# First layer's votes: nine taps in 128 + 32 contraction rows for the upper half of each tile, the seventh share in one PSUM bank, and a new order

## The chip, the cores and the metric

The kernel runs on one core of a Trainium2 chip. The metric is the device time in microseconds (us) of one execution. A core has a tensor engine (PE, with its weight loads listed apart as PEld), a vector engine (DVE), a scalar engine (ACT), GpSimd (POOL) and a sync engine (SP), which only issues transfers here. Each takes its instructions in order from its own queue; engines wait for each other on semaphores. Matrix products land in PSUM, eight banks of 128 x 512 float32; PE writes there, DVE and ACT read from there. All else on chip lies in SBUF.

## The reference, cut to what matters

Four layers, each `x = x + layer(groupnorm(x))` on x of 8 images, 16 channels, 256 x 256 pixels. Only layer 0, a convolution with three rounds of routing, is touched:

```python
w = weights.reshape(kh, kw, cin, atoms * cout)          # 3, 3, 16, 8 * 16
votes = conv_general_dilated(tensor, w, (1, 1), 'SAME')  # 8 * 16 = 128 outputs per pixel
votes = votes.reshape(n, atoms, cout, h, wdt)            # a b c d e, a = image
logits = zeros((a, b, d, e))
for _ in range(3):
    r = softmax(logits, axis=0)                          # over the 8 images
    preds = squash(einsum('abcde,abde->bcde', votes, r), axis=0)
    logits = logits + einsum('abcde,bcde->abde', votes, preds)
return preds
```

Nine taps of 16 channels make 144 contraction rows for 128 outputs. The weighted sum over images, the squash (a norm over the atoms), the dot product with the votes and the softmax over images follow, for every pixel.

## The kernel before, in words

Layer 0 (`layer0`) walks the image in 64 tiles of four rows. A tile has an upper half (h=0, rows 4i and 4i+1) and a lower half (h=1); a half has two rows j; the eight images of a row go in two groups g of four. `prepare` makes the normalised input of a tile: x into `xs`, a product with `wd` (L479, into `pd`), ACT adds the bias (L482, `dn`), and the tile goes to a padded scratch array `d0` in HBM. The output of the first product of a tile lies 128 partitions (8 atoms x 16) by 512 (two rows of 256 pixels) per image, `v[h]`.

Votes before, for both halves: `kt[h]` holds four rows x 16 channels, twice, the second copy shifted by one pixel (dx), so 128 partitions. One call `votes(h, j, g)` makes four images of a row: two matmuls of 128 contraction rows (dx=0 and 1, L533) and two of 64 rows (dx=2, L537; one in each half of the array's rows), into a pair of banks `cv`; ACT copies them to `v` (L542). A row uses three of the four loaded rows, so a quarter of the weights are zeros. Eight calls make a tile: 16 + 16 matmuls.

Then, three times: `squash` (squares on ACT L569, sums over atoms on PE L573, root on ACT L587 to L589, division on DVE L593 to L595, one product on POOL L599 into `f`). After the first two: `logits` for each half: `factor` spreads `f` to 128 rows (PE L617, into a pair of banks `fb`), DVE scales it (L635), multiplies the votes of four and of three images with it (L643, `pr`), PE sums over the output channels (L653, `pl`); `softmax` (transposes L700, L724; DVE L706 to L707 and L716 to L718; exp on ACT L712); `weighted`: PE spreads the shares `rs` of seven images to 128 rows (`rb`, L751: images 4, 5 and 6 in one call, 0 to 3 in another), DVE multiplies them with the votes (L762, `dd`, three pairs and a single one per half), POOL adds up (L771). At the end DVE scales (L813), POOL adds x (L816, `res`), ACT measures sums for the next layer (L828), SP stores (L839, L840, L846 or L848).

What sets the order: layer 0's operations are first recorded, then `_Order.run` writes them out. Each operation has a rank, tile number times a period (61.05) plus an entry of the list `TIMES`; of those whose inputs are recorded as made and whose buffers are free, the lowest rank comes next. The list thus gives priorities, not times: on the chip an instruction starts when its engine and its semaphores let it. About three tiles are in flight. Buffers are counted by kind: three pairs of PSUM banks `x` (for `pd`, `cv`, `fb`, `rb`) and two single banks `u` (for the squash's sums `n2`, `pl`, and the transposes `lg`, `rt`); `kt` has two buffers, `v` six, `dd` four, `io` one (`xs` and `res` share it). Buffers of a kind go round: the next user of a place waits until the last reader of the earlier one is done.

Of the kernel before, what the change touches and what calls it, by code (L numbers as in the profile page):

```python
# [18 lines left out]
P = 128  # L19
WP = W + 2  # L20
# [10 lines left out]
def _consts():  # L31

    p = np.arange(P)
    hi, lo = p // 16, p % 16

    fold = np.stack([h * 16 + lo[:, None] == np.arange(32)[None, :] for h in range(2)], 1)
    unfold = np.zeros((4, 2, C, 2, 4, P), np.float32)
    for h in range(2):
        for k in range(4):
            unfold[k, h, :, h, k] = 0.5 * (np.arange(C)[:, None] == lo[None, :])  # L40


    sel = np.stack([16 * g + 8 * h + hi[:, None] == np.arange(32)[None, :] for g in range(2) for h in range(2)], 1)
    spread = np.zeros((4, 2, 2, 8, 2, 2, 8, C), np.float32)
    for g in range(2):
        for h in range(2):
            for b in range(8):
                spread[:, g, h, b, g, h, b] = 1.0

    diff = np.zeros((B, C, C, B), np.float32)  # L50
    for i in range(C):
        for a in range(B - 1):
            diff[a, i, i, a] = 1.0
            diff[B - 1, i, i, a] = -1.0
        diff[:, i, i, B - 1] = 1.0 / B
    parts = {

        "pair": 0.5 * (p[:, None] // 2 == p[None, :] // 2),
        "diff": diff.reshape(P, P),

        "fold": fold.reshape(P, 2 * 32),
        "unfold": unfold.reshape(P, 8 * P),

        "sel": sel.reshape(P, 4 * 32),

        "spread": spread.reshape(P, 4 * P),
        "ident": np.eye(P),

        "group": (lo[:, None] // 2 == lo[None, :] // 2) / 16.0,

        "same_lo": lo[:, None] == lo[None, :],
        "ones": np.ones((P, P)),
        "mean": np.full((P, P), 1.0 / P),

        "same_c4": lo[:, None] == p[None, :] % 64 // 4,

        "hi8": hi[:, None] == np.arange(8)[None, :],
        "row0": p[:, None] == np.arange(16)[None, :],

        "middle": -(p[:, None] % 4 - 1.5),  # L80

        "pad": _padding(),


        "keep": np.stack([p >= 16, (p < 48) | (p >= 64), p >= 64, p < 64], 1),

        "ident3": _ident3(),
    }
    at = 0
    cols = []  # L90
    for name, a in parts.items():
        a = np.asarray(a, np.float32)
        _CONST[name] = (at, a.shape[1])
        at += a.shape[1]
        cols.append(a)
    return np.ascontiguousarray(np.concatenate(cols, 1))
# [39 lines left out]
def _layout(w0, bw, sw, sc, bias, wq, bq, wk, bk, wv, bv, w3):  # L136
# [1 line left out]


    w0 = w0.reshape(3, 3, C, P)  # L140
    l0 = np.zeros((2, 2, 4, C, 2, P), np.float32)
    for j in range(2):
        for kh in range(3):
            for dx in range(2):
                l0[0, dx, j + kh, :, j] = w0[kh, dx]
                l0[1, dx, j + kh, :, j] = w0[kh, 2]
    l0 = l0.reshape(2, P, 2 * P).transpose(1, 0, 2)


    sw = sw.transpose(1, 4, 2, 3, 0).reshape(C, 2, 4, 81 * C).transpose(0, 2, 1, 3).reshape(64, 2 * 81 * C)  # L150
# [28 lines left out]
class _Buf:  # L179
# [10 lines left out]


TIMES = [
    -723.29, -126.96, -1287.20, -291.27, -719.97, -693.08, -625.75, -683.80, -169.92, -158.78, -153.36,
    -1032.45, -146.30, -286.26, -145.45, -1375.99, -151.90, -338.16, -261.20, -230.76, -136.99, -214.63,
    -126.67, -136.17, -143.63, -139.13, -140.10, -174.81, -899.84, -137.38, -135.05, -211.64, -133.88, -127.93,
    -109.08, -115.69, -139.61, -115.29, -118.15, -149.20, -107.32, -110.73, -165.19, -382.13, -97.75, -92.86,
    -92.25, -91.12, -89.08, -198.43, -88.34, -238.75, -240.66, -85.79, -84.47, -254.75, -133.10, -336.72,
    -223.36, -77.68, -126.26, -82.81, -264.25, -217.14, -78.43, -75.92, -107.53, -72.84, -47.31, -266.51,
    -185.51, -154.67, -555.69, -72.72, -216.04, -93.74, -182.88, -41.32, -30.68, -276.56, -149.62, -123.61,
    -28.12, -118.42, -27.48, -29.71, -88.26, -84.70, -24.63, -62.07, -138.31, -998.81, -338.10, -23.75, -71.35,  # L200
    -168.85, -21.77, -17.87, -1189.68, -15.52, -17.81, -78.48, -11.77, 13.13, -11.07, 16.57, -105.36, -162.33,
    31.16, -216.22, 15.81, 16.90, 16.88, -188.95, 24.25, 29.14, 26.46, 33.82, -255.28, -124.68, -124.23,
    -285.23, -135.30, -169.10, -92.14, -167.00, 36.88, -40.85, -558.24, -220.65, -113.85, -402.73, -159.96,
    35.14, -89.25, 53.60, 71.24, -670.06
]


# [79 lines left out]
class _Net:  # L287
# [123 lines left out]
    def layer0(self, wd, bd, less0, tiles=range(TILES)):  # L411
# [8 lines left out]
        with ExitStack() as st:  # L420
# [1 line left out]
            self.constants(one, "fold", "ident")  # L422
            sbuf = st.enter_context(tc.tile_pool(name="l0_sb", bufs=2))
            psum = st.enter_context(tc.tile_pool(name="l0_ps", bufs=1, space=PSUM))
            w = one.tile([P, 2, 2, P], F32, name="w0")
            nc.sync.dma_start(out=w.rearrange("p s j m -> p (s j m)"), in_=self.d["l0"].rearrange("p s f -> p (s f)"))
            tiny = one.tile([P, 1], F32, name="tiny")
            nc.vector.memset(tiny, 1e-18)
            stats = self.const.tile([P, 2, 2 * TILES], F32, name="st1")
            ident = self.k["ident"]  # L430
            fold = self.k["fold"].rearrange("p (h m) -> p h m", h=2)
            unfold = self.k["unfold"].rearrange("p (h k m) -> p h k m", h=2, k=4)
            sel = self.k["sel"].rearrange("p (g h m) -> p g h m", g=2, h=2)
            spread = self.k["spread"].rearrange("p (g h m) -> p g h m", g=2, h=2)
            ROW = P * WP
# [16 lines left out]
                )  # L452
            nc.sync.dma_start(out=self.d0[(H + 2) * ROW :].unsqueeze(0), in_=ring[0][0:1, 0, 0:16])

            places = dict(io=1, kt=2, v=6, sq=2, f=2, ls=3, e=2, rs=2, s=3, pr=2, dd=4)
            banks = dict(x=3, u=2)
            order = _Order({**places, **banks}, 61.05, TIMES)

            def buf(kind, shape, name=None):
                pool = psum if kind in banks else sbuf  # L460
# [36 lines left out]
            def work(i):  # L497
# [6 lines left out]
                if i + 2 < TILES:  # L504
                    prepare(i + 2, op)

                kt = [buf("kt", [P, 8 * WP]) for _ in range(2)]
                for h in range(2):
                    for dx in range(2):

                        def fetch(h=h, dx=dx):
                            at = (4 * i + 2 * h) * ROW + dx
                            nc.sync.dma_start(
                                out=kt[h]()[dx * 64 : dx * 64 + 64],
                                in_=self.d0[at : at + 4 * ROW].rearrange("(p f) -> p f", f=8 * WP),
                            )

                        op("SP", 0.5, fetch, [("d0", i), ("d0", i + 2 * h - 1)], [(kt[h], dx)], lag=6.0)
                res = buf("io", [P, 2, 512], "res")


                v = [buf("v", [P, 8, 512]) for _ in range(2)]

                def votes(h, j, g):


                    ps = buf("x", [P, 2, 512], "cv")

                    def products():
                        t = kt[h]().rearrange("p (a w) -> p a w", a=8)  # L530
                        for n in range(2):
                            a = 4 * g + 2 * n
                            nc.tensor.matmul(ps()[:, n], w[:, 0, j, :], t[:, a : a + 2, 0:W], start=True, stop=False)  # L533
                        for n in range(2):
                            a = 4 * g + 2 * n
                            at = slice(n * 64, n * 64 + 64)
                            nc.tensor.matmul(  # L537
                                ps()[:, n], w[at, 1, j, :], t[at, a : a + 2, 2 - n : 2 - n + W], start=False, stop=True
                            )

                    def move():
                        nc.scalar.copy(  # L542
                            v[h]()[:, 4 * g : 4 * g + 4, j * W : j * W + W],
                            ps().rearrange("p n (a w) -> p (n a) w", w=W),
                        )

                    op("PE", 3.2, products, [(kt[h], 0), (kt[h], 1)], [(ps, 0), (v[h], "turn")], mode="votes")
                    op("ACT", 1.1, move, [(ps, 0)], [(v[h], g, j)])

                def voted(h, a):  # L550
                    return [(v[h], a // 4, 0), (v[h], a // 4, 1)]

                for g in (1, 0):
                    for h in range(2):
                        for j in range(2):
                            votes(h, j, g)

                def rows(ap):
                    return ap.rearrange("p (r w) -> p r w", w=W)
# [46 lines left out]
                def factor(f, h, also=()):  # L606
# [4 lines left out]
                    def products():  # L611
                        for b in also:
                            b()
                        for n in range(2):
                            for j in range(2):
                                at = slice(64 * j, 64 * j + 64)
                                nc.tensor.matmul(  # L617
                                    fb()[:, j, n * P : n * P + P],
                                    unfold[at, h, 2 * j + n, :],
                                    f()[at, 3],  # L620
                                    start=True,
                                    stop=True,
                                )
# [112 lines left out]
                def weighted(rs):  # L736
# [3 lines left out]
                    for h in range(2):  # L740

                        def term(images, h=h):

                            rb = [buf("x", [P, 2, 512], "rb") for _ in images]

                            def products():
                                for pair, r in zip(images, rb):
# [982 lines left out]
```

## Time and profile before

| what | value |
|---|---|
| time, three runs | median 6453.93 us (6452.06 to 6459.32) |
| profiled execution | 6451.19 us, its span 6448.7 us |
| granted PE clock, mean | 0.989 |
| busy in the span: PE / DVE / ACT / POOL | 6078.3 / 5060.9 / 2967.9 / 3394.3 us |
| votes of layer 0 on PE, first to last | 121.6 to 3369.8 us |
| PE busy, 1000 to 2000 us | 957.96 us |
| DVE busy, 1000 to 2000 us | 894.92 us |
| POOL and ACT busy, 1000 to 2000 us | 759.34 and 423.75 us |
| DMA share and rate, 1000 to 2000 us | 0.37, 96 GB/s |

The profile is one execution on the chip. A row of a table by groups names line, engine, operation, output and input, the number of instructions, their busy time and mean length, then the idle time of the engine ahead of them with what ended it. A float32 matmul shows as two records. Busy shares are means over a stretch; what a stage costs is read from the waits in that stage. Layer 0 repeats with the tile: in a stretch of whole tiles each number divided by the tiles is that of one tile.

### The profile page before, as it was taken

The numbers are of one execution on the slowest core, as the hardware profiler recorded it, in microseconds if no ns is written. First come the engines' busy times: TensorE is split into PE (matmuls) and PEld (weight loads), VectorE is DVE, ScalarE is ACT, GpSimd is POOL, SyncE is SP. The second block draws the span as 40 slices with busy tenths as digits, with TensorE's granted clock in tenths as the row PEclk, the third lists the DMA queues.
The fourth block names the chain that finished last, engine by engine and source line by source line (L and its number), as shares of the span: only waits on it lengthen the run. The fifth ranks groups of instructions, "written<-read, shape, count | busy, mean of one in ns | idle before, by whom it ended". The sixth has DMA issues, their size and how long they took to land.

```text
span 6448.7 us, 109346 instructions
## 1 busy us (share of the span) xinstructions
PE 6078.3 (94%) x44488; PEld 2716.0 (42%) x44488; DVE 5060.9 (78%) x5963; ACT 2967.9 (46%) x4474; POOL 3394.3 (53%) x2464
## 2 busy tenths in 40 slices
PE   2999999999999999999995999999999999999998
PEld 1333333333333333333332444444444566666653
DVE  5788888888888888888886999999999633333331
ACT  0344444444444444444433888888888422112221
POOL 0577777777777777777775434334433211111123
PEclk9999999999999999999996999999999999999999
DMA  7333333333333333333323555555556543434358
GB/s 270 77 94 99 98 98 92 92 98 93 100 96 100 92 92 98 92 101 94 100 69 95 184 180 173 175 178 174 176 180 179 158 82 90 89 83 93 90 176 267
DMA packets 379593, 800.62 MB, mean 124 GB/s; under 512 B 57426, under 2 KB 191154, under 8 KB 343890
## 3 DMA queue, kind: packets, MB, share of 16 engines
q1 hardware_dynamic: 335250, 730.35, 40.4%
q0 software_dynamic: 9856, 29.20, 1.6%
q10 hardware_dynamic: 33984, 34.08, 1.5%
q8 instruction: 349, 5.72, 0.4%
q14 instruction: 154, 1.26, 0.1%
HBM read 582.77 MB, written 210.77 MB: 123 GB/s over the span
## 4 chain that ended last, share of the span: by engine, by line
PE 58%; DVE 32%; issue 4%; DMA 3%; ACT 1%; POOL 1%; SPq 0%; DVEq 0%; POOLq 0%; ACTq 0%
PE cv L533 13%; PE cv L537 7%; PE pqk L1455 7%; DVE bases L1009 7%; PE pl L653 6%; PE rb L751 5%; DVE e L999 4%; DVE pr L643 4%; PE po L1482 4%; DVE dd L762 4%; PE psc L1470 3%; PE pv L1462 3%; PE p L1547 3%; DVE a L999 2%; DVE a L978 2%
## 5 line engine op out<-in xcount | busy, mean ns | idle before, releaser
L771 POOL TENSOR_TENSOR dd<-dd 128x1024 f32<-128x1024 f32 x512 | 1209.0, 2361 | 338.7 <-DVE dd L762 318.4
L1032 PE MATMUL ps<-bases,tw 128*32 128x512 f32 (+1 forms) x13824 | 1361.7, 545 | 16.7 <-POOL bases L1001 6.7
L762 DVE SCALAR_TENSOR_TENSOR dd<-rb,v 128x1024 f32<-128x1024 f32 (+1 forms) x1024 | 1078.0, 1084 | 214.3 <-PE rb L751 175.5
L1001 POOL TENSOR_TENSOR bases<-e,a 128x1024 f32<-128x1024 f32 (+1 forms) x264 | 621.7, 2378 | 928.1 <-DVE e L999 927.8
L542 ACT COPY v<-cv 128x1024 f32<-128x1024 f32 x512 | 518.7, 1013 | 1281.2 <-PE cv L537 1281.2
L643 DVE TENSOR_TENSOR pr<-v,fb 128x2048 f32<-128x2048 f32 (+1 forms) x512 | 1010.9, 2015 | 32.0 <-PE pl L653 28.1
L533 PE MATMUL cv<-kt,w 128*128 128x512 f32 x2048 | 1009.1, 615 | 11.2 <-DMA kt<-d 9.4
L1032 PEld LDWEIGHTS ps<-bases,tw 128*32 128x32 f32 x13824 | 598.2, 109 | 801.7 <-issue 482.9
L771 POOL TENSOR_TENSOR s<-s,dd 128x512 f32<-128x512 f32 x512 | 653.3, 1276 | 30.1
L751 PE MATMUL rb<-rs,ct_fold 32*128 32x512 f32 x3584 | 605.6, 649 | 9.1 <-ACT rs L733 2.4
L533 PEld LDWEIGHTS cv<-kt,w 128*128 128x128 f32 x2048 | 347.0, 189 | 558.8 <-issue 392.7
L537 PE MATMUL cv<-kt,w 64*128 64x512 f32 x2048 | 578.8, 641 | 0.0
L653 PE MATMUL pl<-pr,ct_fold 128*32 128x512 f32 x3584 | 531.6, 605 | 45.4 <-DVE pr L643 45.2
L1466 ACT ACTIVATE vt<-pv,w_b2v 128x128 f32<-128x128 f32 x512 | 146.5, 368 | 840.2 <-PE pv L1462 840.2
L771 POOL TENSOR_TENSOR s<-v,dd 128x512 f32<-128x512 f32 x256 | 325.9, 1273 | 340.0 <-DVE dd L762 330.9
L1455 PE MATMUL pqk<-w_qk,t 128*128 128x512 f32 x1024 | 482.9, 594 | 4.7 <-POOL t L1449 4.6
L1487 DVE TENSOR_TENSOR y<-po,res 128x512 f32<-128x512 f32 x128 | 88.5, 691 | 493.9 <-PE po L1482 468.5
L1009 DVE SCALAR_TENSOR_TENSOR bases<-xr,xm,bases 128x1024 f32<-128x1024 f32 (+1 forms) x264 | 447.9, 1734 | 0.3 <-POOL bases L1001 0.3
L1449 POOL TENSOR_TENSOR t<-t,emb 128x512 f32<-128x512 f32 x128 | 162.5, 1270 | 514.0 <-DVE t L1445 494.3
L986 ACT ACTIVATE sq<-a 128x1024 f32<-128x1024 f32 (+1 forms) x264 | 263.7, 999 | 231.4 <-DVE a L978 230.7
L968 ACT ACTIVATE d<-xr,bd,sd 128x1024 f32<-128x1024 f32 (+1 forms) x264 | 319.0, 1208 | 14.1 <-DMA xr<-x1p 14.1
L751 PEld LDWEIGHTS rb<-rs,ct_fold 32*128 32x128 f32 x3584 | 173.0, 185 | 351.0 <-issue 118.2
(269 smaller groups left out, 8430.3 us busy)
## 6 DMA issues: line engine op xcount, KB each, us to landing
kt<-d SPq DMA_DIRECT2D x256, 516.0 KB
xr<-x1p SPq DMA_DIRECT2D x120, 1024.0 KB
d<-dn ACTq DMA_DIRECT2D x64, 516.0 KB
x<-y SPq DMA_DIRECT2D x128, 258.0 KB
xs<-in_x_dram SPq DMA_DIRECT2D x16, 2048.0 KB
xs<-in_x_dram SPq DMA_DIRECT2D x64, 512.0 KB
res<-in_x_dram SPq DMA_DIRECT2D x64, 512.0 KB
x<-s SPq DMA_DIRECT2D x128, 256.0 KB
```

The costliest lines, as they stand in the source:

```text
L533: nc.tensor.matmul(ps()[:, n], w[:, 0, j, :], t[:, a : a + 2, 0:W], start=True, stop=False)
L537: nc.tensor.matmul(ps()[:, n], w[at, 1, j, :], t[at, a : a + 2, 2 - n : 2 - n + W], start=False, stop=True)
L542: nc.scalar.copy(v[h]()[:, 4 * g : 4 * g + 4, j * W : j * W + W], ps().rearrange("p n (a w) -> p (n a) w", w=W),)
L643: nc.vector.tensor_tensor(pr()[:, :n].rearrange("p n (r w) -> p n r w", w=W), v[h]()[:, 4 * g : 4 * g + n].rearrange("p n (r w) -> p n r w ...
L653: nc.tensor.matmul(pl()[at : at + 32], sel[:, g, h, :], pr()[:, t, :], start=h == 0 and g == 0, stop=h == 1 and (g == 1 or t == 3),)
L751: nc.tensor.matmul(r()[:, n], spread[at, g, h, :], rs()[at], start=True, stop=True)
L762: nc.vector.scalar_tensor_tensor(dd()[:, :n], r()[:, :n], 1.0 / B, v[h]()[:, a : a + n], ALU.subtract, ALU.mult)
L771: op("POOL", us, lambda: nc.gpsimd.tensor_tensor(out[0](), a[0](), b[0](), ALU.add), a[1] + b[1], out[1])
L1001: nc.gpsimd.tensor_tensor(ring[n % 3][:, 0, p : p + m, 1 : 1 + W], rows(e), rows(a), ALU.subtract)
L1009: nc.vector.scalar_tensor_tensor(r, rows(part[1]), xm[:, b : b + 1], v, ALU.is_gt, ALU.mult)
L1032: nc.tensor.matmul(out if k is None else out[:, k], lhs, rhs, start=start, stop=stop, skip_group_check=True)
L1455: nc.tensor.matmul(ps, t[:, n, k * P : (k + 1) * P], wqk[:, n, :], start=n == 0, stop=n == 1)
```

## The change

Three things change in layer 0; the other layers are the same.

1. The upper half's votes. `kt` is now made per row j: partitions 0 to 95 hold three taps of dx=0 and three of dx=1, 96 to 127 two taps of dx=2 (16 channels each). A second, small buffer `kr` holds what the ninth tap needs, in four groups of 32 partitions, each with the two images of one matmul; half of the weights' rows there are zeros. The ninth tap's four matmuls of 32 rows come first and start all four banks of two `x` pairs (operation `rest`); then the eight taps' matmuls of 128 rows add to them (`most`, two per pair). The lower half keeps the old form under the name `votes_wide`. Fetches of the upper half per tile: six (two of 96 partitions, two of 32, two of `kr`) in place of two of 64.
2. The weighted sum's seventh image takes one `u` bank (`r6`) in place of a pair `x`.
3. Period and `TIMES` are new (49), and votes of a tile are recorded half by half.

The unused half of the constant `unfold` is dropped and the weight array `l0` carries both forms.

```diff
-            places = dict(io=1, kt=2, v=6, sq=2, f=2, ls=3, e=2, rs=2, s=3, pr=2, dd=4)
+            places = dict(io=1, kt=2, kr=2, v=6, sq=2, f=2, ls=3, e=2, rs=2, s=3, pr=2, dd=4)
             banks = dict(x=3, u=2)
-            order = _Order({**places, **banks}, 61.05, TIMES)
+            order = _Order({**places, **banks}, 49, TIMES)
...
+                def votes(h, j):
+                    kt = buf("kt", [P, 8 * WP])
+                    kr = buf("kr", [P, 2 * WP])
+                    at = (4 * i + 2 * h + j) * ROW
...
+                    def fetch():
+                        rows_at(kt()[:96], 0, [[1, 2], [8 * WP, 48], [1, 8 * WP]])
+                    def fetch2():
+                        rows_at(kt()[96:], 2, [[8 * WP, 32], [1, 8 * WP]])
+                    def fetch3():
+                        rows_at(kr(), 16 * 8 * WP + 2, [[2 * WP, 4], [8 * WP, 32], [1, 2 * WP]])
...
+                    ps = [buf("x", [P, 2, 512], "cv") for _ in range(2)]
+                    def most(g):
+                        t = kt().rearrange("p (a w) -> p a w", a=8)
+                        for n in range(2):
+                            a = 4 * g + 2 * n
+                            nc.tensor.matmul(ps[g]()[:, n], w[:, 0], t[:, a : a + 2, 0:W], start=False, stop=True)
+                    def rest():
+                        for g in range(2):
+                            for n in range(2):
+                                at = slice(64 * g + 32 * n, 64 * g + 32 * n + 32)
+                                t = kr()[at].rearrange("p (a w) -> p a w", a=2)[:, :, 0:W]
+                                nc.tensor.matmul(ps[g]()[:, n], w[at, 1], t, start=True, stop=False)
...
-                for g in (1, 0):
-                    for h in range(2):
+                for h in range(2):
+                    if h in (0,):
                         for j in range(2):
-                            votes(h, j, g)
+                            votes(h, j)
+                    else:
+                        wide(h)
...
-                            rb = [buf("x", [P, 2, 512], "rb") for _ in images]
+                            rb = [buf("x", [P, 2, 512], "rb") if len(a) == 2 else buf("u", [P, 1, 512], "r6") for a in images]
```

`wide(h)` fetches one `kt` of the old form and calls `votes_wide(h, kt, j, g)`, whose matmuls and ACT copy are those of the old `votes`.

## The prediction

> **What bounds the kernel now.** I read the page first, for the stage, then one stretch of layer 0 (1000 to 3000 us) by its waits, then one tile in order of time. The slices:
>
> ```profile
> PE   2999999999999999999995999999999999999998
> ...
> DVE  5788888888888888888886999999999633333331
> ...
> DMA  7333333333333333333323555555556543434358
> ```
>
> Layer 0 is the long flat part: PE at 9, DVE at 8, transfers at 3. How long is a tile? 2000 us hold 39 runs of L482 (one per tile): 51.28 us. PE is busy 957.96 of 1000 us, 49.1 us per tile, so 2.15 idle; DVE 894.92, 45.9, so 5.4 idle. Neither is full: they wait for each other. The waits of that stretch, in us over 39 tiles (total, times, longest):
>
> ```profile
> DVE dd L762 <- PE rb L751: 94.0, 136, 1.3
> DVE s L813 <- PE fb L617: 62.1, 39, 1.6
> DVE dd L762 <- POOL dd L771: 19.2, 39, 0.5
> DVE pr L643 <- PE pl L653: 18.2, 77, 0.3
> PE rt L724 <- DVE e L718: 29.1, 39, 0.8
> PE pl L653 <- DVE pr L643: 22.6, 40, 0.6
> PE pd L479 <- DVE dd L762: 19.6, 36, 0.9
> ```
>
> DVE loses 2.4 us per tile waiting for spread shares, 1.6 for the last factor; PE loses 1.9 us waiting for DVE. So a saving on PE is worth only what the loop through both engines lets through. Lengths come from one tile in order of time (start, length, engine, line; in brackets idle time and releaser):
>
> ```profile
> 2003.97 1.98 PE L533 MATMUL cv<-kt,w 128*128 128x512 f32 x4
> 2005.89 1.13 PE L537 MATMUL cv<-kt,w 64*128 64x512 f32 x4
> 2006.85 0.61 PE L617 MATMUL fb<-f,ct_fold 64*128 64x128 f32 x8
> 2025.23 1.13 PE L751 MATMUL rb<-rs,ct_fold 32*128 32x512 f32 x6
> 2026.29 1.98 PE L533 MATMUL cv<-kt,w 128*128 128x512 f32 x4
> ...
> 2026.52 1.82 DVE L762 SCALAR_TENSOR_TENSOR dd<-rb,v 128x512 f32<-128x512 f32 x2 [0.95 <-PE rb L751]
> 2028.26 0.28 DVE L593 SCALAR_TENSOR_TENSOR f<-n,f 128x128 f32<-128x128 f32 x1
> ...
> 2038.84 1.14 PE L751 MATMUL rb<-rs,ct_fold 32*128 32x512 f32 x8
> ```
>
> Start to next start counts, since ends overlap: two 128-row matmuls 1.92 us, the two 64-row ones together 0.96 to 1.06, a group of three or four 32-row ones 1.07, a factor 0.54. From the start of a spread to DVE's first use of it: 2026.52 - 2025.23 = 1.29 (1.24 to 1.29 elsewhere).
>
> **The votes.** Per upper row j, before, two calls of two 128-row and two 64-row matmuls: 2 x (1.92 + 1.06) = 5.96 us. After: the ninth tap's four matmuls of 32 rows, by the row of L751, 1.07, and two pairs of 128 rows, 3.84: 4.91. Saved 1.05 per row, 2.1 us per tile. PE's work falls from 49.1 to 47.0 per tile. Were PE alone the bound with the same idle time, 61 steady tiles (L482 runs from about 230 to 3370 us) would give 128 us.
>
> [...] The trace's own row has four in 1.07 (3.6x): I take 1.07. [...]
>
> **The transfers.** Bytes per tile for votes, from 8,256 bytes per partition of `kt`: before 4 x 64 partitions, 2.11 MB; after 2 x 128 + 128 partitions and 2 x 128 x 2,064 bytes of `kr`, 3.70 MB. The rate goes from 96 to about 128 GB/s, the share from 0.37 to about 0.5; the page shows 0.5 and 180 GB/s in layer 1, so there is room. Issues on SP rise from 11 or 12 to 15 or 16 per tile at about 0.5 us each: SP stands idle most of a tile. Is any late? `kt` keeps two buffers for three users per tile now. In the new order the lower half's `kt` may be fetched when the second upper row's last matmul is done and is wanted 16 us later (counted below: 15.6 to 31.5); the second row's has 18 us. A `kt` piece took 8.3 us to land in the chain at the layer's start, two behind each other about 9. Cover 6 us or more: cost nothing; without that cover each us late is a us per tile on PE. The next tile's x (`xs`) is now issued ahead of the stores instead of after them and has 10 us. At the layer's start two more issues ahead of the first votes: 1 us.
>
> **The pair rule of PSUM.** `rest` needs two of three `x` pairs at once, and the spreads of four images also take two. In return the seventh share leaves `x` for `u`. Whether that stalls depends on the order; I read it from the built program, which repeats exactly by tile, with the semaphore each instruction waits for, and followed the chain through it.
>
> **The new order, by its chain.** DVE lengths, start to start: pair `dd` 1.135, single 0.60, scale 0.67, `pr` of four images 2.25, of three 1.70, squash 1.33, first part of a softmax 1.40, second 1.91. A handoff DVE or ACT to PE is 0.05. Time 0: PE starts the first factor of a tile's first round.
>
> 1. PE: factor 0.54, `pd` 1.82, a wide vote 2.97, 5.33; shares are spread, DVE can use them at 5.33 + 1.27 = 6.60. DVE, meanwhile done with scale and both `pr`, stands since 5.65: gap 0.95.
> 2. Three `dd` pairs and a single, 4.0: 10.6. Scale, `pr`, squash, `pr`: 6.0: 16.6.
> 3. The next spread takes the bank pair of that factor, so PE, done with `rest` and `most` at 15.55, waits till 16.65, and DVE then waits for the spread: 1.34, to 17.95. Both engines stand here in turn.
> 4. `dd` 4.0: 21.95. Scale, softmax part, `pr`, softmax part, `pr`: 7.93: 29.9. PE waits 0.85 for the last.
> 5. Scale, two `pr`, squash: 5.95: 35.85. POOL's product (0.15 + 0.45 + 0.1), the factor until DVE's start 0.65 (2016.40 to 2017.05 in the trace of before): 37.25, gap 1.4. In before this wait was 1.6.
> 6. Two final scales while PE makes the second factor and a spread, usable at 36.6 + 1.05 + 1.27 = 38.9: gap 0.4. `dd` pair, pair, single 2.87, softmax part 1.4, pair 1.135: 44.3; the single of the other half is ready at 44.55: gap 0.25.
> 7. Single, pair, softmax part, squash, pair: 6.1: 50.7. The next tile's first factor takes this pair's banks: period 50.7.
>
> Gaps: 0.95 + 1.34 + 1.4 + 0.4 + 0.25 = 4.3 us per tile; the listed DVE waits of before, with small ones, came to 5.2. PE has 3.7 us idle, more than before: its saving of 2.1 us goes mostly into waiting. The move of the seventh share costs nothing: its `u` bank is free in time everywhere in this chain (n2's group waits for it at 45.2 and comes at 45.5), under cover of PE's `pd`, votes and factors. POOL is nearest to being late: a `dd` buffer it frees at 44.9 is wanted at 45.2; 0.3 us of cover, beyond which each tenth is a tenth per tile.
>
> **Sum.** (51.28 - 50.7) x 61 = 35 us, less 1 at the start: 34. Profiled execution 6451.2 - 34 = 6417; the median of the runs lies 2.7 above the profiled one: 6420. Ends of the unknowns: the chain's lengths are good to some 0.05 at each of about ten handoffs, so 50.2 to 51.2 per tile: 6389 to 6450.
>
> **Rivals.**
>
> - *PE's saving comes through whole.* For it: PE is at 96%. If the gaps on DVE shrink with PE's work, the period is 51.28 - 2.1 = 49.2: 6454 - 128 = 6326. Against it: DVE's 45.9 plus the handoffs that no order avoids (the last squash to final scale, 1.4; one ping-pong, 1.3) is 48.6 already, and the new order has three more. Halfway, 49.9, gives 6370.
> - *Nothing to see.* The new gaps sum to the old ones: 51.1 to 51.5, within 0.2% (13 us, about what the spread of the three runs lets one tell). For it: my sum is 0.6 us per tile better on 50, and the chain has ten handoffs.
> - *Slower: POOL's buffer.* Place: the single and pair `dd` after step 6 wait for places that POOL's additions free. POOL's chain there is final sum 1.27, two final adds 2.5, a pair add 2.4, a single 1.25, all behind the squash at 35.85. If these run later than I read, the `dd` waits; before showed such a wait 39 times in 39 tiles (0.5 each). From 0.3 us late it costs one for one; at 1.1 us late the gain is gone, at 1.3 the kernel is slower by over 0.2%; 1.6 us late means 52.0: 6454 + 44 = 6498. Against it: POOL is busy 759 of 1000 us and has no longer additions than before.
> - *A transfer comes late*: beyond 16 us for the lower half's `kt`; 17 us would be 51.7: 6480. Against it: 9 us seen. [...] the trace shows 0.09 us at the most (two 128-row matmuls take 1.92 ahead of 64-row ones, 1.82 as `pd` ahead of 128-row ones), and the new form makes fewer such changes.
>
> **How the numbers follow.** Forecast 0.45; whole or half of PE's saving 0.12; nothing to see 0.15; POOL's buffer or longer gaps of that kind 0.20; transfer 0.08. Faster: 0.45 + 0.12, and a little from the forecast's upper end goes to no change: 0.58. Same: 0.16. Slower: 0.26. The likeliest case's own range is 6389 to 6450. To leave out 2 in 10, the range goes down to the halfway case, 6370, and up to 6485, which takes in the transfer at 17 us and most of POOL's case.
>
> **What would show it.** In the profile after: the ninth tap's four matmuls start to start in 1.07 and the pairs of the eight taps at 1.92; PE busy near 925 of 1000 us, DVE near 905; tiles every 50.7; the spread of step 3 waiting about 1 us for DVE `pr`; the last factor's DVE wait at 1.4; no PE wait for `kt`; transfers at a share near 0.5. I am wrong if PE's waits for DVE stay at 1.9 per tile (then PE's saving came through), if `dd` waits for POOL grow past 1 us per tile, or if votes wait for a transfer.

## The result

The changed kernel takes 6827.5 us (median of four runs, 6821.17 to 6834.1); the kernel before took 6455.55 beside it (6452.06 to 6459.32). The ratio is 1.0576, 95% interval 1.0558 to 1.0594: 5.8% slower, where 6420 was forecast and 6370 to 6485 given as range. All of it is in layer 0. From one run of L486 (`pd`, the old L479) to that 35 tiles later are 1982.02 us in the changed kernel's trace, 56.63 per tile; before, 2002.84 us for 39 tiles, 51.36. The difference of 5.27 over the 64 tiles is 337 us of the 372. Another 17 us are at the layer's start, where the prediction had put 1: the first fetch takes 25.65 us in the chain of the changed kernel and took 8.32 before, so the first eight-tap matmuls start at 138.4 us, where the votes before started at 121.6. The sums that follow layer 0 start at 3864.6 us in place of 3492.3, 372 us later; after layer 0 nothing is lost.

The waits of the changed kernel between 1000 and 3000 us (engine, line, what ended the wait: total us, times, longest), some 35 tiles:

```profile
PE cv L548 <- DMA kt<-d: 150.2, 35, 5.6
...
DVE fb L705 <- PE fb L687: 194.9, 36, 7.0
...
DVE s L883 <- PE fb L687: 80.9, 36, 2.3
...
DVE dd L832 <- PE rb L821: 56.0, 71, 1.8
PE rb L821 <- DVE pr L713: 41.9, 35, 1.2
```

The first line did not exist before: once per tile the eight-tap matmuls of the second upper row (L548) stand 4.3 us for their `kt`. DVE then waits 5.5 us per tile for the factor that PE makes after these matmuls (L705 <- L687). The last three are handoffs that the prediction had counted, the first of them at 1.4 us and here 2.2.

One such tile in order of time, PE's rows and SP's issues (SPq) about it:

```profile
1987.01 1.09 SPq L527 DMA_DIRECT2D kt<-d  x2
...
2003.36 1.42 PE L555 MATMUL cv<-kr,w 32*128 32x512 f32 x8
2008.93 6.33 PE L548 MATMUL cv<-kt,w 128*128 128x512 f32 x8 [4.14 <-DMA kt<-d]
...
2049.12 1.20 PE L555 MATMUL cv<-kr,w 32*128 32x512 f32 x8
2050.25 3.70 PE L548 MATMUL cv<-kt,w 128*128 128x512 f32 x8
```

The fetch goes out at 1987.0 and its data are used at 2008.9. And the four matmuls that waited take 6.33 us, where the four of the first upper row, without a wait, take 3.70. The same stretch cut in pieces (stretch, length; busy us and instructions of PE, PEld, DVE, ACT and POOL; granted PE clock, DMA share, GB/s) shows more of both:

```profile
1990.00:1993.00 3.00, 3.00 (x42) 1.40 (x35) 2.90 (x4) 1.20 (x3) 2.95 (x2) 1.00 0.10 41
...
2005.00:2008.00 3.00, 0.00 (x0) 0.00 (x0) 3.00 (x3) 0.58 (x1) 3.00 (x2) 0.91 0.20 76
2008.00:2009.50 1.50, 0.57 (x1) 0.50 (x2) 1.43 (x3) 0.00 (x0) 1.42 (x2) 0.50 0.23 84
...
2019.00:2022.00 3.00, 2.91 (x21) 1.13 (x16) 3.00 (x4) 1.16 (x4) 0.00 (x0) 1.00 0.12 52
```

While the fetch runs and little else does, the DMA share is 0.10 at 41 GB/s. Another stretch with only such a fetch, 2019 to 2022 us, has 0.12 at 52 GB/s. Of the 16 DMA engines that the share counts this is the time of 1.6 to 1.9 (an estimate from the shares); which ones a transfer uses the trace does not name. And the clock granted to PE falls in the wait: in steps of 0.5 us it is 0.50 from 2007.5 to 2014.0 us, over most of the matmuls that come next. Per tile that is 4.25 us of waiting and 2.4 us of slow matmuls (16 records of L548 per tile at a mean of 755 ns instead of the 605 that the runs below show), 6.6 us. The tile ought thus to have taken 50 us.

### The profile page after: what moved, and what is told of

Read it like the earlier page. It is cut to its first block, busy times and chain, and to the rows that moved or that the text cites. A ratio compares the mean times of both kernels' runs of the same rounds, so it can differ in the third digit from the quotient of the medians.

```text
span 6819.4 us, 110134 instructions
## 1 busy us (share of the span) xinstructions
PE 6105.1 (90%) x44488; PEld 2802.2 (41%) x44488; DVE 5049.7 (74%) x5963; ACT 2971.2 (44%) x4474; POOL 3393.0 (50%) x2464
## 4 chain that ended last, share of the span: by engine, by line
PE 45%; DVE 25%; DMA 23%; issue 5%; ACT 2%; POOL 1%; SPq 0%; DVEq 0%; POOLq 0%; ACTq 0%
DMA kt<-d 21%; PE pqk L1525 6%; DVE bases L1079 6%; PE cv L548 6%; PE cv L585 5%; DVE e L1069 4%; PE po L1552 4%; PE pv L1532 3%; PE psc L1540 3%; PE p L1617 3%; PE cv L589 3%; PE rb L821 3%; PE pl L723 3%; DVE dd L832 3%; PE fb L687 2%
## 5 line engine op out<-in xcount | busy, mean ns | idle before, releaser
L1102 PE MATMUL ps<-bases,tw 128*32 128x512 f32 (+1 forms) x13824 | 1359.6, 545 | 17.7 <-POOL bases L1071 7.9
L832 DVE SCALAR_TENSOR_TENSOR dd<-rb,v 128x1024 f32<-128x1024 f32 x768 | 904.6, 1212 | 109.8 <-PE r L821 61.7
L548 PE MATMUL cv<-kt,w 128*128 128x512 f32 x1024 | 615.0, 756 | 324.4 <-DMA kt<-d 324.4
L821 PE MATMUL rb<-rs,ct_fold 32*128 32x512 f32 x3072 | 574.7, 632 | 87.2 <-DVE pr L713 73.3
L669 POOL TENSOR_TENSOR f<-f 128x128 f32<-128x128 f32 x192 | 87.8, 458 | 907.7 <-DVE f L665 903.3
L548 PEld LDWEIGHTS cv<-kt,w 128*128 128x128 f32 x1024 | 238.8, 246 | 694.6 <-issue 661.2
L723 PE MATMUL pl<-pr,ct_fold 128*32 128x512 f32 x3584 | 508.0, 604 | 8.9 <-DVE pr L713 8.7
L585 PE MATMUL cv<-kt,w 128*128 128x512 f32 x1024 | 495.2, 606 | 10.0 <-DMA kt<-d 1.1
L821 PEld LDWEIGHTS rb<-rs,ct_fold 32*128 32x128 f32 x3072 | 215.7, 186 | 384.5 <-issue 226.2
```

The source lines that it names most:

```text
L548: nc.tensor.matmul(ps[g]()[:, n], w[:, 0], t[:, a : a + 2, 0:W], start=False, stop=True)
L585: nc.tensor.matmul(ps()[:, n], w2[:, 0, j, :], t[:, a : a + 2, 0:W], start=True, stop=False)
L723: nc.tensor.matmul(pl()[at : at + 32], sel[:, g, h, :], pr()[:, t, :], start=h == 0 and g == 0, stop=h == 1 and (g == 1 or t == 3),)
L821: nc.tensor.matmul(r()[:, n], spread[at, g, h, :], rs()[at], start=True, stop=True)
L832: nc.vector.scalar_tensor_tensor(dd()[:, :n], r()[:, :n], 1.0 / B, v[h]()[:, a : a + n], ALU.subtract, ALU.mult)
L1102: nc.tensor.matmul(out if k is None else out[:, k], lhs, rhs, start=start, stop=stop, skip_group_check=True)
```

## The experiments

**One fetch made two, of 48 partitions each.** Same bytes, same `kt`, every instruction of PE, DVE, ACT and POOL in the same place.

```diff
-    rows_at(kt()[:96], 0, [[1, 2], [8 * WP, 48], [1, 8 * WP]])
+    for dx in range(2):
+        rows_at(kt()[48 * dx : 48 * dx + 48], dx, [[8 * WP, 48], [1, 8 * WP]])
```

> The changed kernel with its 96-partition fetch issued as two transfers of 48 partitions, one per shift, same bytes, same order on every compute engine. Theory A: the transfer with a leading dimension of 2 [...] (in the trace of the changed kernel the DMA share stays at 0.11 to 0.12 with about 55 GB/s for some 14 us of each tile) and so takes about 21 us to land, where the order leaves 18. Split, each part [...] lands in 8 to 10 us: no PE wait for kt, the tile falls to the 50.7 us of the chain in the prediction, time 6400 to 6440. Rival B: the fetch is late because kt has two buffers for three users and SP has more to issue: then the wait stays, time within 1% of 6827. Rival C: the data come in time but the new order itself is slower than the old: 6460 to 6600, without a PE wait for kt.

6393.76 us (6389.63 to 6406.66), ratio to before 0.991 (0.9893 to 0.9926). 434 us come back, and the change is now faster than the kernel before by 0.9%; the time is a little below the 6400 to 6440 expected. The tile takes 50.35 us (1963.67 us for 39 tiles). Its waits, in the same stretch and columns as above (lines moved by one):

```profile
DVE dd L833 <- PE rb L822: 63.8, 80, 1.8
DVE s L884 <- PE fb L688: 59.9, 40, 1.5
PE rb L822 <- DVE pr L714: 47.9, 40, 1.2
DVE dd L833 <- PE r L822: 40.3, 40, 1.0
PE pl L724 <- DVE pr L714: 28.1, 40, 0.7
PE fb L688 <- DVE dd L833: 27.5, 39, 0.7
```

No wait for `kt` is left, nor does DVE wait for the factor behind it. B falls (SP issues one transfer more per row than in the changed kernel, with the same two buffers) and C falls.

A second execution of this kernel, on the chip used for the next experiment and for the last one, gives an idea of the spread: 6398.01 us.

> A second look at the kernel with two fetches, beside the kernel with the loops turned round on the same chip: 6385 to 6410 by every theory; it tells how far two chips or two looks differ.

**One fetch, its two loops turned round.** Perhaps two fetches help for being smaller. Here it is one, of 774 KB as in the changed kernel; only the order of its dimensions is another.

```diff
-    rows_at(kt()[:96], 0, [[1, 2], [8 * WP, 48], [1, 8 * WP]])
+    rows_at(kt()[:96], 0, [[8 * WP, 48], [1, 2], [1, 8 * WP]])
...
-    l0[0] = np.concatenate(taps[:8])
+    l0[0, :96] = np.stack([w0[:, 0], w0[:, 1]], 2).reshape(96, P)
+    l0[0, 96:] = np.concatenate(taps[6:8])
```

> The changed kernel with the two loops of its 96-partition fetch turned round: leading dimension 48 (row and channel), then the two shifts, in place of the two shifts and then 48; the weights' first 96 rows are put in the matching order. One transfer as in the changed kernel, the same bytes in the same 8,256-byte pieces, every instruction on every engine in the same place. Theory A: [...] the fetch lands in time and the time is that of the kernel with two fetches, 6385 to 6405. Rival: the two fetches helped because they are smaller or queue differently; then one transfer of 774 KB stays late, 6780 to 6830.

6395.47 us (6391.94 to 6396.58), ratio 0.9904 (0.989 to 0.9919): the whole effect. The fetch whose outer dimension is 2 is late here, and the one with 48 is not: the second row's goes out at 2002.40 us in this trace and is used at 2020.11, 17.7 us later and without a wait, where the changed kernel has 21.9 (1987.01 to 2008.93). Nothing else differs but the order of the rows in `kt` and in the weights that goes with it. Why the outer dimension does this, no run shows. No wait for `kr`, whose outer dimension is 4, is listed in this run between 1000 and 3000 us.

**The kernel before, with such a fetch.** If an outer dimension of 2 makes a fetch late there too, the old kernel must suffer as well.

```diff
-    at = (4 * i + 2 * h) * ROW + dx
-    nc.sync.dma_start(
-        out=kt[h]()[dx * 64 : dx * 64 + 64],
-        in_=self.d0[at : at + 4 * ROW].rearrange("(p f) -> p f", f=8 * WP),
-    )
+    at = (4 * i + 2 * h) * ROW
+    src = self.d0[at : at + 1]
+    if not dx:
+        nc.sync.dma_start(
+            out=kt[h](),
+            in_=bass.AP(tensor=src.tensor, offset=src.offset, ap=[[1, 2], [8 * WP, 64], [1, 8 * WP]]),
+        )
```

> The kernel before with each half's kt fetched by one transfer whose leading dimension is 2 (both shifts, 64 partitions each) in place of two transfers of 64 partitions; nothing else. Theory A: 1.06 MB [...] at about 55 GB/s are 19 us, two per tile are 38 us [...], so they land after the 25 us or so that the order leaves: PE waits for kt, 6550 to 7000. Rival B: fewer issues and the same bytes, so nothing changes or it is a little faster: 6440 to 6460.

6896.14 us (6893.94 to 6903.1), ratio 1.0687 (1.0671 to 1.0703): within the range of A, with half the issues. But not where it was expected:

```profile
DVE fb L639 <- PE fb L621: 233.1, 34, 9.3
PE pd L479 <- DMA xs<-in_x_dram: 182.9, 32, 7.6
```

(its waits, 1000 to 3000 us). `kt` is in time; the tile's x is late, 5.7 us per wait, a transfer that the edit does not touch, and DVE waits for the factor that PE makes behind those products. The share of DMA time fell from 0.37 to 0.24 at the same time. In one such tile the store that SP issues ahead of x takes 4.34 us to issue, where it took 1.09 to 1.22 before, and from the end of x's own issue (2009.76) to its first use (2018.72) are 8.96 us, where two in the chain of before took 7.80 and 8.03 to land. How the fetches of `kt` hold x back is not shown: no run separates one reason from another, so the cause stays open. The `pd` matmuls after this wait are slow too, a mean of 1072 ns per record against 618 before; the granted clock from 1000 to 3000 us is 0.94, before it was 1.00.

**The votes in the old form, in the new order.** What is the 144-row form worth by itself? From the kernel with two fetches, the upper half's matmuls go back to two 128-row and two 64-row ones for each four images, at the same places.

```diff
-    nc.tensor.matmul(ps[g]()[:, n], w[:, 0], t[:, a : a + 2, 0:W], start=False, stop=True)
+    nc.tensor.matmul(ps[g]()[:, n], w2[:, 0, j, :], t[:, a : a + 2, 0:W], start=False, stop=True)
...
-    at = slice(64 * g + 32 * n, 64 * g + 32 * n + 32)
-    t = kr()[at].rearrange("p (a w) -> p a w", a=2)[:, :, 0:W]
-    nc.tensor.matmul(ps[g]()[:, n], w[at, 1], t, start=True, stop=False)
+    a = 4 * g + 2 * n
+    at = slice(64 * n, 64 * n + 64)
+    nc.tensor.matmul(
+        ps[g]()[:, n], w2[at, 1, j, :], t[at, a : a + 2, 2 - n : 2 - n + W], start=True, stop=False
+    )
```

> The new order and the seventh share in one bank, but the upper half's votes computed in the old form: per row two fetches of 64 partitions into kt, first the dx=2 taps as 64-row matmuls into both pairs of banks, then the 128-row ones; the ninth-tap fetch is dropped. The compute engines' order is that of the changed kernel, instruction for instruction, except the shape of these matmuls. PE has 1.05 us more per upper row. Theory A with the chain of the prediction: PE stands 1.1 us at the step where it waits for pr, so nearly all is absorbed, 0.2 to 0.4 us per tile remain: 10 to 30 us over the kernel with the two fetches. Rival: PE sets the time, then 2.1 us per tile, 128 us over it.

6407.16 us (6405.32 to 6416.5), ratio to before 0.9931 (0.9916 to 0.9945); the tile takes 50.63 us (1974.47 for 39). Against 6393.76 the form is worth 13 us (the ranges of the runs overlap a little, so its size is rough; the traces give 0.28 us per tile). The PE work between the two is not the 2.1 us per tile of the expectation. The old form first, then the second upper row of the kernel with two fetches:

```profile
1013.34 1.99 PE L553 MATMUL cv<-kt,w 64*128 64x512 f32 x8
1015.26 3.70 PE L545 MATMUL cv<-kt,w 128*128 128x512 f32 x8
...
2026.30 1.42 PE L556 MATMUL cv<-kr,w 32*128 32x512 f32 x8
2027.65 3.70 PE L549 MATMUL cv<-kt,w 128*128 128x512 f32 x8
2031.28 1.07 PE L724 MATMUL pl<-pr,ct_fold 128*32 128x512 f32 x8
```

Start to next start, the four 64-row matmuls, put together here, take 1.92 us in either row; the four of 32 rows take 1.35 in the second row and 1.13 in the first. That is 1.4 us per tile (1.7 by the busy time: 965.92 us of 1000 in the old form and 938.18 in the new, while DVE has 901.90 and 906.39). Two waits of PE for `pr`, those of steps 3 and 4, shrink from 1.2 and 0.7 us per tile to 0.4 and almost nothing when PE has more to do: most of the saving had gone into them. The rival, that PE sets the time, is out: it would now ask for some 87 us instead of 128, and 13 came. What is left between this run and the kernel before, 48 us, belongs to the new list and the moved share together; the last two experiments try each without the other.

**The seventh share alone, in the old order.**

```diff
-    rb = [buf("x", [P, 2, 512], "rb") for _ in images]
+    rb = [buf("x", [P, 2, 512], "rb") if len(a) == 2 else buf("u", [P, 1, 512], "r6") for a in images]
```

> The kernel before with the seventh share in one bank of the kind u instead of a pair of the kind x, list and period as before. Theory: pairs come free earlier, u is used more, the rest of the order hardly moves: 6440 to 6470, within 0.2% of before. Rival: u, with two banks for one more user, makes PE wait: over 6470.

6688.13 us (6684.7 to 6692.81), ratio 1.0364 (1.0348 to 1.0379). A miss of 220 us. Its waits on PE for the squash's sums:

```profile
PE n L573 <- DVE dd L762: 76.8, 36, 2.3
PE n L573 <- ACT rs L733: 25.0, 37, 0.7
```

`u` goes round through two banks. With the share in it, the sums `n2` (L573) must wait until DVE has read the share: 2.1 us per tile, and 0.7 us at another place; the last factor's wait on DVE grows from 1.6 to 3.1 us (113.0 over 36). The tile takes 54.95 us.

**The seventh share back in a pair, in the new order.** The same line undone in the kernel with two fetches.

> The kernel with two fetches, but the seventh share back in a pair of the kind x; list and period those of the change, so the order is what the new list makes with the old buffers. In the old order the move of the share cost 233 us because the squash's sums stand behind it in u. Theory: the new list is made for the share in u and gives pairs away at places where there are none now; slower than 6394 by 50 to 300 us. Rival: the move is a burden in any order and without it the time falls below 6390.

7297.11 us (7285.45 to 7301.82), ratio 1.1304 (1.1285 to 1.1323), 64.85 us per tile. Worse still, and far above the expected 50 to 300 us:

```profile
DVE dd L833 <- PE rb L822: 529.0, 185, 9.6
PE fb L688 <- POOL f L670: 182.1, 62, 5.7
```

Without the `u` bank the list places spreads and factors otherwise; PE stands at a factor for POOL while the spreads that DVE needs are queued behind it. List and buffers hang together: each list with the other's buffers costs 233 to 903 us.

## Why the prediction was wrong

- **The step that failed is "The transfers".** It took the 8.3 us that a fetch of 516 KB needed at the layer's start for a fetch of another shape (the new one took 25.65 at that very place), and said "Cover 6 us or more: cost nothing". For the second row's fetch the cover was put at 18 us, about what the order gave; the fetch took 21.4 to land. The bytes, the rate of 128 GB/s (measured 130 with the fetches in order) and the free share were right. What was missing is the outer dimension of the fetch: at the 41 to 52 GB/s of the trace, 774 KB take some 15 to 19 us (an estimate), and the one that was late took 21.4 beside others.
- **The price of a late fetch was too low as well.** "Each us late is a us per tile on PE" leaves out what follows the wait: 4.25 us of waiting drew 2.4 us of slow matmuls behind it. In the tile shown the granted clock is down to 0.50 at 2007.5 us, 2.7 us after PE's last matmul ended (2004.78).
- **The rival named it, at the wrong place.** "A transfer comes late" was given 0.08 and tied to the lower half's `kt`, at 17 us; it was the upper half's second row. That votes wait for a transfer was among the prediction's signs of being wrong.
- **The chain stood.** With the fetch mended the tile takes 50.35 us where 50.7 was summed, and the kernel 6394 us where 6420 was forecast. (Before, the tile took 51.36; the prediction had 51.28 by dividing 2000 us by 39.) One tile of DVE in that kernel, its idle times in brackets:

```profile
2011.08 1.22 DVE L833 SCALAR_TENSOR_TENSOR dd<-rb,v 128x1024 f32<-128x1024 f32 x1 [1.00 <-PE r L822]
...
2022.45 0.69 DVE L833 SCALAR_TENSOR_TENSOR dd<-r,v 128x512 f32<-128x512 f32 x1 [1.42 <-PE rb L822]
...
2041.58 1.28 DVE L884 TENSOR_TENSOR s<-s,fb 128x512 f32<-128x512 f32 x2 [1.50 <-PE fb L688]
2043.03 2.35 DVE L833 SCALAR_TENSOR_TENSOR dd<-rb,v 128x1024 f32<-128x1024 f32 x2 [0.16 <-PE rb L822]
```

  Steps 1, 3, 5 and 6 had 0.95, 1.34, 1.4 and 0.4. PE's own waits, 1.1 in step 3 and 0.85 in step 4, were 1.20 and 0.70.
- **The ninth tap** was met as a sum, by luck. Its four matmuls take 1.13 us in the first upper row (2049.12 to 2050.25 in the changed kernel) but 1.35 in the second, in the mean 1.24, not the 1.07 of L751; why the rows differ is open. The four matmuls of 128 rows behind them take 3.63 us, not 3.84, so that a row costs 4.76 to 4.98 where 4.91 was summed. It hardly mattered, as the prediction said: 13 us for the form against the old one in the same order. One reading beside it was misplaced: two 128-row matmuls were read as some 0.09 us longer ahead of 64-row ones (1.92) than ahead of 128-row ones (1.82), but before the change two of them took 1.82 us ahead of 64-row ones too, where a transpose of 128 rows stood in front (2048.99 to 2050.81).
- **"The move of the seventh share costs nothing"** holds in the new order, where the sums' wait for the share does not show, and only there: alone in the old one it costs 233 us.
- **POOL's buffer** as a rival is out: in the kernel with two fetches no wait of DVE for POOL is listed between 1000 and 3000 us.

## What to carry to other kernels

Read the shape of a transfer before its size: a tile filled by one transfer whose outer loop runs over two copies went at 41 to 52 GB/s here, and the same bytes with the loops turned round came without a wait. A wait on PE can be dearer than its length: 4.25 us per tile drew 2.4 more here, with the granted clock down to 0.50. And a list of priorities belongs to the buffers it was made for: judge a change of buffers and list together, and follow the chain through both engines to see what a saving on one of them is worth.

## What the runs showed of the hardware

- In one tile of the changed kernel a fetch of 96 partitions from a source with outer dimension 2 took 21.42 us to land, and where little else ran the DMA share was 0.10 to 0.12; with outer dimension 48 the same bytes were used 17.7 us after their issue, without a wait.
- Where the slow fetch is may not be where the wait is: in the old kernel with such fetches PE waited 5.7 us at a time for x, which was fetched as before, and not for `kt`. How the one delays the other is not shown.
- In the tile shown PE stood from 2004.78 to 2008.93 us, its granted clock was 0.50 from 2007.5 to 2014.0, and four matmuls took 6.33 us instead of 3.70. That the clock alone makes them slow is not shown: at the layer's start of the changed kernel four of them took 6.35 us behind 20.55 us of standing, and the view lists a clock of 1.00 there.
